# A graph network with a mixture of experts: all rows of the last stage scattered in parts of 40 and 9 tiles, expert weights packed in DRAM, and larger zero fills

## The chip, the cores and the metric

The kernel runs on one core of one Trainium2 chip. The metric is the device time of one execution in microseconds (us), and the figure for a version is the median of its runs. Version before: 4450.49 us, median of three runs between 4450.0 and 4450.73.

## What is computed

The reference takes 6250 nodes with 256 features and a sorted list of 106,250 edges (each node also has an edge to itself). Four blocks follow one another, each of the form x = x + block(layernorm(x)):

```python
x = x + _L0_gnn_ref(_layernorm(x), edge_index, ...)   # two GIN layers, hidden width 512
x = x + _L0_ffn_ref(_layernorm(x)[None], ...)[0]      # slice attention over 64 tokens and 8 heads
x = x + _L1_gnn_ref(_layernorm(x), edge_index, ...)   # one GCN layer with a folded batch norm
x = x + _L1_ffn_ref(_layernorm(x)[None], ...)[0]      # mixture of experts
```

A graph layer sums the rows of the source nodes over the edges of each target node. The mixture of experts is the part that the change is about:

```python
gate_logits = x_flat @ Wg + bg + bias
topk_vals, topk_idx = jax.lax.top_k(gate_logits, TOP_K)          # 2 of 8 experts
topk_w = jax.nn.softmax(topk_vals, axis=-1)
combine = (jax.nn.one_hot(topk_idx, NUM_EXPERTS, dtype=x.dtype) * topk_w[..., None]).sum(axis=1)
h = jax.nn.relu(jnp.einsum('td,edh->teh', x_flat, W1) + b1)      # 256 -> 512
y = jnp.einsum('teh,ehd->ted', h, W2) + b2                       # 512 -> 256
out = jnp.einsum('ted,te->td', y, combine)
```

## The kernel before

The nodes are cut into NT = 49 tiles of 128 rows (the last has 106), the edges into 831 chunks of 128, 17 of them for each tile.

**Sums over edges.** Three times a table in DRAM (T1, T2, T3) holds each node's row as three bf16 pieces. The class `Sums` (L176 to L228) goes over the tiles: for each chunk GpSimd (POOL) issues an indirect DMA that gathers the 128 source rows into a ring of message buffers (L152; 10 buffers in the first and third sum, 32 in the second), with at most `FLIGHT` = 5 on their way, and TensorE (PE) multiplies them with a 0/1 matrix `hot` made by VectorE (DVE, L194), in three matmuls per chunk (L173). Other work is put between these matmuls by hand: `between` gives seven slots per tile.

**Stage 1** (gin1, L635 to L683) is the first sum with the two dense layers of the first GIN layer, for four tiles at a time. Beside it SP, the queue that issues plain DMAs in order, stores the results (S2 at L674, T2 at L680) and fills buffers in DRAM with zeros (L605 to L646): the accumulators S3 and the buffers XD of the experts' rows. Each fill is 512 KB in four slices of one row of zeros per partition, and each waits for a sum that has been added (`added`), so that the fills are spread over the stage.

**Stage 2** (L738 on) is the second GIN layer with the statistics of the attention, then a short dense part. In it `third_needs` (L715) brings the experts' biases b1 into columns and stores them as B1 in DRAM (L728).

**Stage 3** (L965 on) is the GCN sum with the mixture of experts beside it. Its order on SP, PE, ACT and DVE is that of the program text (`manual_schedule`), and `in_order` keeps the order of gathers on POOL. For every two tiles `choice` (L1004) computes the layer's result, normalises it, picks the two experts, and ranks the rows by a matmul with a triangular matrix (pp, L1075), so that each row gets two places in XD, which has a region for each expert. `send` (L1090) scatters the rows there by four indirect DMAs on POOL (L1094). `advance` (L1118) works out on DVE which blocks of 128 rows of one expert are now full, and writes expert and first row of each block into `which`.

A block is fetched by `fetched` (L1170): SP loads two registers from `which`, then issues the loads of xd (128 rows), and by `weights_of` (L1159) those of W1 (512 KB), W2 (512 KB), b1 (2 KB) and b2 (128 KB), up to `AHEAD` = 4 blocks ahead. `block_of` (L1206) transposes xd (L1221), `products` (L1189) does 8 matmuls for the hidden layer (ph, L1195; ReLU with b1 on ACT, L1197) and 4 for the output (py, L1202; b2 added on DVE, L1203), and SP stores the block in its place in XD (L1229). (The profile lists each of these f32 matmuls twice.) A block is done in two slots.

The tiles are divided into parts with XD buffers of their own. When all blocks of a part are done, `combine` (L1253) gathers each row's two results (two indirect DMAs g per tile, L1260, with L152 in the profile) and DVE adds them with their shares (L1265); then the tile goes to `out` (L1002). Parts before: tiles 0 to 35 with 79 blocks and tiles 36 to 47 with 31. How many blocks an expert has is known only when the kernel runs, so the numbers are upper bounds. The last tile is not scattered: it is multiplied with all eight experts ("dense", L1208 to L1217) and each result is added with the row's share, which may be zero.

After the last sum (L1343 on) the remaining blocks follow one another, with one tile combined in each half block.

Of the kernel before, what the change touches and what calls it, by code (L numbers as in the profile page):

```python
# [17 lines left out]
P = 128  # L18
# [3 lines left out]
def gin_transolver_gcn_moe(ctx: ExitStack, tc: tile.TileContext, a: dict, out: bass.AP):  # L22
# [33 lines left out]
    assert C == G == 64 and KD * P == D and KH * P == HID and NT <= P and HID <= 512 and 2 * D <= 512  # L56
# [317 lines left out]
    for upto, size in ((0.75, P), (1.0, P)):  # L374
        ts = [t for t in range(sum(map(len, parts)), NT - 1) if (t + 0.5) / (NT - 1) <= upto]
        if ts:
            parts.append(ts)
            Bs.append(size)
# [4 lines left out]
    zeros = const.tile([P, 1, D], F32, name="zeros")  # L383
# [7 lines left out]
    with tc.tile_pool(name="own", bufs=1) as own:  # L391
# [201 lines left out]
        with tc.tile_pool(name="g1w", bufs=1) as wp, \  # L593
# [12 lines left out]
            for xd in XD:  # L606
                n = xd.shape[0] // P
                for q in range(0, n, 4):
                    m = min(4, n - q)
                    fills.append((xd[q * P:(q + m) * P, :].rearrange("(p j) f -> p j f", p=P), m))  # L610

            for q in range(0, NT, 4):
                m = min(4, NT - q)
                fills.append((S3[q:q + m].rearrange("j p f -> p j f"), m))
# [20 lines left out]
            def gin1(ts):  # L635
                J = len(ts)
                T = J * P
                for t in ts:
                    added = sums1.added
                    for _ in range(-(-len(fills) // (NT - t))):  # L640
                        at, m = fills.pop()
                        ins = nc.sync.dma_start(at, zeros.to_broadcast([P, m, D]))
                        tc.add_manual_dep(ins.ins, added.ins.name,
                                          mybir.DependencyInfo(mybir.DependencyClass.Sync,
                                                               mybir.DependencyReason.DATA),
                                          reason="spread over the stage")  # L646
# [41 lines left out]
    B1 = dram.tile([NE, P, KH], F32, name="B1")  # L688
# [26 lines left out]
    def third_needs(w, ps):  # L715
# [12 lines left out]
        nc.sync.dma_start(B1.rearrange("e p k -> p e k"), b1.rearrange("p (e k) -> p e k", k=KH))  # L728
# [261 lines left out]
    share = keep.tile([P, NE], F32, name="share")  # L990
# [13 lines left out]
    def choice(i, ts, sent_at):  # L1004
# [57 lines left out]
        if i is None:  # L1062
            shares()
            dense.append(xT)
            nc.vector.tensor_scalar(share, pick[0][:, 0, :], sh[:, 0, 0:1], None, op0=OP.mult)
            nc.vector.scalar_tensor_tensor(share, pick[1][:, 0, :], sh[:, 0, 1:2], share, op0=OP.mult, op1=OP.add)
            return


        both = w.tile([P, 4, NE], F32, name="both")  # L1070
        nc.vector.tensor_add(both[:, :J, :], pick[0][:, :J, :], pick[1][:, :J, :])
# [18 lines left out]
    def send(i, ts, xn):  # L1090

        for j, t in enumerate(ts):
            for c in range(2):
                ins = nc.gpsimd.indirect_dma_start(  # L1094
                    out=XD[i], out_offset=bass.IndirectOffsetOnAxis(ap=place[:, t, c:c + 1], axis=0),
                    in_=xn[:, j, :], in_offset=None)
# [62 lines left out]
    def weights_of(e):  # L1159
        W1 = ew.tile([P, KD, HID], F32, name="W1", bufs=AHEAD)  # L1160
        nc.sync.dma_start(W1, a["L1_ffn_W1"][e].rearrange("o (k p) f -> p (o k) f", p=P))
        W2 = ew.tile([P, KH, D], F32, name="W2", bufs=AHEAD)
        nc.sync.dma_start(W2, a["L1_ffn_W2"][e].rearrange("o (k p) f -> p (o k) f", p=P))
        b1 = ew.tile([P, KH], F32, name="b1e", bufs=AHEAD)
        nc.sync.dma_start(b1, B1[e].rearrange("o p k -> p (o k)"))
        b2 = ew.tile([P, 1, D], F32, name="b2e", bufs=AHEAD)
        nc.sync.dma_start(b2[:, 0, :], a["L1_ffn_b2"][e].to_broadcast([P, D]))
        return W1, W2, b1, b2

# [19 lines left out]
    def products(xdT, W1, W2, b1, b2):  # L1189
# [13 lines left out]
        nc.vector.tensor_tensor(yd, p[:, :D], b2[:, 0, :], op=OP.add)  # L1203
        yield yd

    def block_of(i, got):  # L1206

        if i is None:  # L1208
            e, got = got
            it = products(dense[0], *got)  # L1210
            next(it)
            yield
            yd = next(it)
# [170 lines left out]
```

## Time and profile before

The profile comes from one execution with the hardware profiler on, which has a time of its own.

| What | Value |
|---|---|
| Median of the runs without profiler | 4450.49 us |
| Profiled execution: own time | 4515.05 us |
| Profiled execution: span | 4513.4 us |
| Mean granted TensorE clock | 0.817 |
| Stage 1 / stage 2 / attention, about | 100 to 1345 / 1345 to 2700 / 2700 to 2776 us |
| Stage 3: sums / the rest after them | 2776 to 4300 / 4300 to 4513 us |
| Busy: PE, PE loads, DVE, ACT, POOL | 69%, 45%, 34%, 17%, 57% of the span |
| DMA queue q0 (indirect, from POOL) | 182,064 packets, 678.86 MB, 47.8% of 16 engines |
| DMA queue q1 (plain, from SP) | 308,656 packets, 353.08 MB, 24.0% of 16 engines |

A group of instructions is shown as line, engine, operation, what is written and read, shape and count, then busy time in us and the mean of one in ns, then the idle time of the engine before them and what ended it. "PEld" is TensorE loading weights; a name with q (SPq, ACTq) is the engine's own queue of waits and DMA issues, which does not count as busy. "issue" is waiting for nothing that the profile shows. In a timeline each line has start and length in us, and in brackets how long the engine had been idle and for whom. DMA packets are recorded singly in the trace with queue, start, size and duration.

### The profile page before, as it was taken

Reading aid. Unit: us, or ns where it says so; the run is one execution under the profiler, and the core shown is the slowest. Engines: PE = TensorE matmul, PEld = TensorE weight load, DVE = VectorE, ACT = ScalarE, POOL = GpSimd, SP = SyncE. Lnnn points to the kernel's source line nnn. Section 1 sums busy time; section 2 is a strip of 40 time slices with the busy share of each in tenths; the row PEclk is TensorE's granted clock in tenths of the full one; section 3 lists DMA queues with packets and bytes.
Section 4 is the critical chain, followed back from the end, with each engine's and each line's share of the span. In section 5 each row is a group of like instructions: output and inputs, shape, how many; then the busy total and the mean of one; then the engine's idle time right before and its main releaser. Section 6 shows DMA issues by size and latency. Waiting matters only on the chain. (4 is left out here: it accounts for less than half of the span.)

```text
span 4513.4 us, 45778 instructions
## 1 busy us (share of the span) xinstructions
PE 3133.2 (69%) x14516; PEld 2025.4 (45%) x14592; DVE 1532.2 (34%) x3891; ACT 788.2 (17%) x1496; POOL 2578.6 (57%) x2719
## 2 busy tenths in 40 slices
PE   2577777777874777878767876566666666677567
PEld 1233343433442444434434454345555555566456
DVE  6122222222231433433434454333333332333332
ACT  4011111111120111111111123011212221122122
POOL 3666666666646666666666502665665555555642
PEclk6688888888987898988989977677778777788779
DMA  6676666666668888888888755467766676687678
GB/s 210 190 227 215 215 197 206 210 214 208 195 210 289 296 295 301 304 293 289 297 289 292 248 165 178 136 189 220 225 206 207 216 222 215 215 263 219 194 239 257
DMA packets 497447, 1044.56 MB, mean 231 GB/s; under 512 B 79469, under 2 KB 294607, under 8 KB 497200
## 3 DMA queue, kind: packets, MB, share of 16 engines
q0 software_dynamic: 182064, 678.86, 47.8%
q1 hardware_dynamic: 308656, 353.08, 24.0%
q10 hardware_dynamic: 6480, 9.63, 0.6%
q8 instruction: 117, 1.92, 0.2%
q14 instruction: 130, 1.06, 0.1%
HBM read 878.42 MB, written 162.92 MB: 231 GB/s over the span
## 5 line engine op out<-in xcount | busy, mean ns | idle before, releaser
L152 POOL DMA_INDIRECT msg<-T,srcT x2493 | 2359.7, 947 | 1682.4 <-issue 763.0
L173 PE MATMUL pa<-msg,hot 128*128 128x256 bf16 (+2 forms) x7404 | 1492.0, 342 | 540.7 <-DMA msg<-T,srcT 395.1
L173 PEld LDWEIGHTS <-hot 128*128 128x128 bf16 x7479 | 804.8, 108 | 1142.0 <-issue 742.6
L1195 PE MATMUL ph<-xdT,W 128*128 128x128 f32 x1760 | 287.4, 315 | 197.6 <-ACT hT L1197 85.6
L194 DVE SCALAR_TENSOR_TENSOR hot<-dstT,node 128x1152 bf16<-128x1152 f32 (+2 forms) x297 | 373.1, 1258 | 23.8 <-PE pa L173 12.9
L1195 PEld LDWEIGHTS ph<-xdT,W 128*128 128x128 f32 x1760 | 252.8, 219 | 232.5 <-ACT hT L1197 97.5
L1202 PE MATMUL py<-W,hT 128*128 128x256 f32 x944 | 264.9, 425 | 25.4 <-issue 13.8
L622 DVE TENSOR_TENSOR dinv<-dinv,pa 128x1 f32<-128x1 f32 x145 | 22.3, 153 | 714.2 <-PE pa L173 460.8
L1197 ACT ACTIVATE hT<-ph,b1e 128x128 f32<-128x128 f32 x472 | 165.9, 367 | 449.7 <-remote 161.9
L835 PE MATMUL ptok<-xn,sw 128*128 128x257 f32 (+1 forms) x392 | 125.1, 458 | 157.1 <-DVE sw L827 63.7
L670 PE MATMUL p<-W2a,h2T 128*128 128x512 f32 x392 | 199.8, 651 | 33.9 <-issue 18.0
L1202 PEld LDWEIGHTS py<-W,hT 128*128 128x128 f32 x944 | 190.5, 215 | 64.8 <-issue 22.6
L663 PE MATMUL p<-h1T,W1b 128*128 128x512 f32 (+2 forms) x448 | 204.0, 599 | 19.5 <-ACT h1T L657 13.1
L835 PEld LDWEIGHTS ptok<-xn,sw 128*128 128x128 f32 (+1 forms) x392 | 84.8, 227 | 195.7 <-issue 74.7
L152 POOL DMA_INDIRECT g<-XD,place x96 | 93.8, 977 | 125.0 <-DMA XD<-yd 54.8
L1203 DVE TENSOR_TENSOR yd<-py,b2e 128x256 f32<-128x256 f32 x118 | 49.9, 423 | 306.6 <-PE py L1202 177.4
L1015 PE MATMUL pn<-Wg,sT 128*128 128x256 f32 x196 | 82.2, 592 | 83.6 <-issue 44.6
L655 PE MATMUL p<-h0T,W1a 128*128 128x512 f32 (+2 forms) x224 | 129.8, 711 | 7.3 <-issue 4.0
L663 PEld LDWEIGHTS p<-h1T,W1b 128*128 128x128 f32 x448 | 87.5, 212 | 103.8 <-issue 83.2
L670 PEld LDWEIGHTS p<-W2a,h2T 128*128 128x128 f32 x392 | 78.0, 211 | 121.6 <-issue 103.7
L1094 POOL DMA_INDIRECT XD<-xn,place x96 | 94.7, 986 | 62.5 <-issue 46.1
L235 DVE TENSOR_TENSOR s<-s,pa 128x512 f32<-128x512 f32 x49 | 33.6, 685 | 269.0 <-PE pa L173 146.7
(306 smaller groups left out, 3059.6 us busy)
## 6 DMA issues: line engine op xcount, KB each, us to landing
W<-in_L_ffn_W SPq DMA_DIRECT2D x236, 512.0 KB
XD<-zeros SPq DMA_DIRECT2D x100, 512.0 KB
msg<-T,srcT POOLq DMA_INDIRECT x2493
T<-tp SPq DMA_DIRECT2D x49, 384.0 KB
b2e<-in_L_ffn_b SPq DMA_DIRECT2D x118, 128.0 KB
xd<-XD SPq DMA_DIRECT2D x110, 128.0 KB
XD<-yd SPq DMA_DIRECT2D x110, 128.0 KB
S<-s SPq DMA_DIRECT2D x49, 256.0 KB
```

Of the source, the lines that this page charges most:

```text
L152: return nc.gpsimd.indirect_dma_start(out=msg, out_offset=None, in_=table, in_offset=bass.IndirectOffsetOnAxis(ap=ix, axis=0))
L173: nc.tensor.matmul(pa[:, :n], hot, msg[:, s * F:s * F + n], start=(start and s == 2), stop=(stop and s == 1))
L194: nc.vector.scalar_tensor_tensor(hot[:, :n, :], dstT[:, c0:c0 + n, None].to_broadcast([P, n, P]), float(k * HALF), node2[:, k % 2, None, : ...
L655: nc.tensor.matmul(p[:, :T], W1a[:, k, m * P:(m + 1) * P], h0T[:, k, :T], start=(k == 0), stop=(k == KD - 1))
L663: nc.tensor.matmul(p[:, :T], W1b[:, k, m * P:(m + 1) * P], h1T[:, k, :T], start=(k == 0), stop=(k == KH - 1))
L670: nc.tensor.matmul(p, h2T[:, k, j * P:(j + 1) * P], W2a[:, k, :], start=(k == 0), stop=(k == KH - 1))
L835: nc.tensor.matmul(p[:, :D + 1], sws[j][:r, m * P:(m + 1) * P], xn[:r, j, :], start=(j == 0), stop=(j == J - 1))
L1015: nc.tensor.matmul(p[:, :D], sT[:, k, j * P:(j + 1) * P], Wg3[:, k, :], start=(k == 0), stop=(k == KD - 1))
L1094: ins = nc.gpsimd.indirect_dma_start(out=XD[i], out_offset=bass.IndirectOffsetOnAxis(ap=place[:, t, c:c + 1], axis=0), in_=xn[:, j, :], in ...
L1195: nc.tensor.matmul(p[:, :P], W1[:, k, m * P:(m + 1) * P], xdT[:, k, :P], start=(k == 0), stop=(k == KD - 1))
L1197: nc.scalar.activation(hT[:, m, :], p[:, :P], AF.Relu, bias=b1[:, m:m + 1])
L1202: nc.tensor.matmul(p[:, :D], hT[:, m, :], W2[:, m, :], start=(m == 0), stop=(m == KH - 1))
```

## The change

Three things are changed.

First, the parts: all 49 tiles are scattered now, 40 in the first part and 9 in the second, and the dense last tile goes (with it the code for `i is None`). The parts have 87 and 25 blocks. The last tile's 106 rows are ranked, scattered and gathered with slices of 106, and rows past the end are cleared in `both`. What was after the last sum becomes one loop, in which the chains of choices, the last scatters, the blocks and the combining go on side by side.

Second, the weights: in stage 1, for one tile in four, `packed` loads one expert's W1, W2 and b2 (repeated for all partitions) into a buffer and stores it as rows of `EW` = 2308 floats (9,232 bytes) per partition in a DRAM buffer WB. The columns of b1 go to the end of these rows in stage 2, instead of B1. A block's four loads become one load of WB.

Third, the fills: the row of zeros gets four times as long, and each partition fills one contiguous piece of 4 KB instead of four of 1 KB.

```diff
-    for upto, size in ((0.75, P), (1.0, P)):
-        ts = [t for t in range(sum(map(len, parts)), NT - 1) if (t + 0.5) / (NT - 1) <= upto]
+    for upto, size in ((0.81, P), (1.0, P)):
+        ts = [t for t in range(sum(map(len, parts)), NT) if (t + 0.5) / NT <= upto]
...
-    zeros = const.tile([P, 1, D], F32, name="zeros")
+    EW = KD * HID + KH * D + D + KH
+    WB = dram.tile([NE, P, EW], F32, name="WB")
+    zeros = const.tile([P, 4 * D], F32, name="zeros")
...
-                    fills.append((xd[q * P:(q + m) * P, :].rearrange("(p j) f -> p j f", p=P), m))
+                    fills.append((xd[q * P:(q + m) * P, :], m))
...
-                fills.append((S3[q:q + m].rearrange("j p f -> p j f"), m))
+                fills.append((S3[q:q + m].rearrange("j p f -> (j p) f"), m))
+            def packed(e, added):
+                t = w.tile([P, EW - KH], F32, name="wb", bufs=2)
+                for at, ap in (
+                        (t[:, :KD * HID].rearrange("p (k f) -> p k f", f=HID),
+                         a["L1_ffn_W1"][e].rearrange("(k p) f -> p k f", p=P)),
+                        (t[:, KD * HID:EW - KH - D].rearrange("p (k f) -> p k f", f=D),
+                         a["L1_ffn_W2"][e].rearrange("(k p) f -> p k f", p=P)),
+                        (t[:, EW - KH - D:], a["L1_ffn_b2"][e:e + 1].to_broadcast([P, D]))):
+                    spread(nc.sync.dma_start(at, ap), added)
+                nc.sync.dma_start(WB[e][:, :EW - KH], t)
...
-                        ins = nc.sync.dma_start(at, zeros.to_broadcast([P, m, D]))
...
+                        spread(nc.sync.dma_start(at.rearrange("(p j) f -> p (j f)", p=P), zeros[:, :m * D]), added)
+                    if t % 4 == 2 and t // 4 < NE:
+                        packed(t // 4, added)
...
-        nc.sync.dma_start(B1.rearrange("e p k -> p e k"), b1.rearrange("p (e k) -> p e k", k=KH))
+        nc.sync.dma_start(WB.rearrange("e p f -> p e f")[:, :, EW - KH:], b1.rearrange("p (e k) -> p e k", k=KH))
...
-        W1 = ew.tile([P, KD, HID], F32, name="W1", bufs=AHEAD)
-        nc.sync.dma_start(W1, a["L1_ffn_W1"][e].rearrange("o (k p) f -> p (o k) f", p=P))
-        W2 = ew.tile([P, KH, D], F32, name="W2", bufs=AHEAD)
-        nc.sync.dma_start(W2, a["L1_ffn_W2"][e].rearrange("o (k p) f -> p (o k) f", p=P))
-        b1 = ew.tile([P, KH], F32, name="b1e", bufs=AHEAD)
-        nc.sync.dma_start(b1, B1[e].rearrange("o p k -> p (o k)"))
-        b2 = ew.tile([P, 1, D], F32, name="b2e", bufs=AHEAD)
-        nc.sync.dma_start(b2[:, 0, :], a["L1_ffn_b2"][e].to_broadcast([P, D]))
-        return W1, W2, b1, b2
+        wb = ew.tile([P, EW], F32, name="wb", bufs=AHEAD)
+        nc.sync.dma_start(wb, WB[e].rearrange("o p f -> p (o f)"))
...
-    last, = chains
-    for _, *rows in to_send:
-        send(*rows)
-    due.extend(fresh)
-    due.extend((None, e) for e in range(NE))
-    while due or ready or pending[0] is not None:
-        next(last, None)
+    while chains or to_send or due or ready or pending[0] is not None:
+        for it in list(chains):
+            if next(it, chains) is chains:
+                chains.remove(it)
+        if to_send:
+            send(*to_send.pop(0)[1:])
+            new_blocks()
         next(block_pieces)
         if to_combine:
             combine(now[0] + 2)
```

`spread` adds the dependency on `added` that the fills had before. Lines in the profile of the changed kernel are some 3 to 20 higher than before.

## The prediction

> **What bounds the kernel now.** I read the granted clock first (0.817 over the span), then the busy time by stretch, the groups of the last stage, and the timelines of its tail. Columns of the first view: stretch, length, busy us (instructions) of PE, PEld, DVE, ACT, POOL; then clock, DMA share, GB/s.
>
> ```profile
> 400.00:700.00 300.00, 223.26 (x889) 117.96 (x888) 75.05 (x139) 35.48 (x56) 193.68 (x205) 0.85 0.68 210
> 3000.00:3200.00 200.00, 135.83 (x731) 107.80 (x732) 66.81 (x238) 37.78 (x85) 114.47 (x121) 0.75 0.69 213
> 4300.00:4450.00 150.00, 108.47 (x541) 89.40 (x538) 42.75 (x135) 40.35 (x107) 56.46 (x58) 0.81 0.80 247
> ```
>
> No engine is full in stage 1 (100 to 1345 us), the MoE loop (2776 to 4300) or the tail (4300 to 4513). The loop's groups show a coupling instead:
>
> ```profile
> L152 POOL DMA_INDIRECT msg<-T,srcT x829 | 785.1, 947 | 568.4 <-PE pa L173 271.8 <-issue 175.2 <-remote 53.7
> L173 PE MATMUL pa<-msg,hot 128*128 128x256 bf16 x2492 | 433.5, 326 | 224.6 <-DMA msg<-T,srcT 152.0 <-issue 35.6 <-DMA s<-S 21.1
> L1195 PE MATMUL ph<-xdT,W 128*128 128x128 f32 x1424 | 229.2, 312 | 166.3 <-ACT hT L1197 74.7 <-issue 71.7 <-DVE xr L1020 11.4
> ```
>
> POOL waits 272 us for PE to free the ten message buffers, PE 152 us for messages, and 166 us inside expert blocks, mostly behind ACT's ReLU. That ReLU has a wait of its own, for b1's DMA:
>
> ```profile
> L1197 ACTq EVENT_SEMAPHORE x118: 17/1326/10824, 2952.3 to 4495.4; - x118
> ```
>
> Summed over the trace's records it is 208 us for the loop's blocks, 40 us for the tail's. b1 is the fourth of five loads of a block (xd, W1, W2, b1, b2) on SP's queue.
>
> The starts of L1328 give the pace: tile pairs 10 to 39 take 62.3 us on average, with 4 blocks and 38 POOL operations each (34 gathers, 4 scatters; 0.95 us and a 0.30 gap each, 47.5 us). Pairs 40-43 have 7 blocks each and take 61.2 us: three more blocks cost nothing. Pairs 44-47 have 4 blocks, but 14 combining gathers between them, and take 76.3 and 69.1 us. So the loop follows POOL's list, and a block is nearly free in it.
>
> In the tail 29 blocks remain after the last sum at 4300.3: 21 scattered, 8 of the dense last tile. With nothing beside them blocks go at 5.13 us (timeline of PE, then of POOL):
>
> ```profile
> 4442.40 1.99 PE L1202 MATMUL py<-W,hT 128*128 128x256 f32 x8
> 4447.53 1.99 PE L1202 MATMUL py<-W,hT 128*128 128x256 f32 x8
> ...
> 4498.74 1.89 PE L1202 MATMUL py<-W,hT 128*128 128x256 f32 x8
> ```
>
> ```profile
> 4465.18 0.94 POOL L152 DMA_INDIRECT g<-XD,place  x1 [54.76 <-DMA XD<-yd]
> ...
> 4503.66 1.00 POOL L152 DMA_INDIRECT g<-XD,place  x1 [0.30 <-DVE xr L1265]
> ```
>
> The last 24 combining gathers start when the last scattered block's store has landed and run beside the dense blocks; both finish together, near 4500.
>
> **The change, part by part.** Sums are made against the profiled execution (span 4513.4, own time 4515.05). The median without profiler is 4450.49, 1.4% less; I carry the difference in us over unchanged.
>
> *Parts 40 and 9.* Counting the instruction order of both versions: 118 blocks become 112; 88 lie in the loop either way, plus one in the last tile, so the tail falls from 29 to 23. All 98 combining gathers now lie in the tail (before, 18 of 96 lay in tiles 44-48). Pairs 44-47 then have 7 blocks and no combining, as 40-43 had: 145.4 - 2 x 61.2 = **-23 us** (from -10, if the two slow pairs were slow for another reason, to -28 with tile 48's four).
>
> Tail, from the last sum T. The first three blocks end at T+37 before, paced by the last tile's chain; I keep that. The last tile is now scattered. Its ranking matmul follows block 3 (T+36). Placing took 1.5 us on DVE for the previous pair, and from the first scatter to SP's fetch of a final block 14.3 us (4303.5 to 4317.7). So its 16 final blocks can be fetched near T+53 and be there by T+58. Seven blocks, three loaded and four due from pair 46-47, run meanwhile to about T+61: hidden, by 3 us only. Behind the waiting fetch on SP stand the weight loads, output stores and block stores, so a late chain costs its lateness once, 5 to 10 us.
>
> Combining 40 tiles of part one at two per block takes 20 blocks. Such blocks now go at 6.9 us (7 in the 48 us to 4405). SP takes about 7 us for each (eight issues of 0.6, plus 2 of register loads), the DMA engines 6.2 by the packet records. Their undisturbed packets are 46 ns for 1 KB, 84 for 2, 121 for 3, 159 for 4, 178 for 4.6, 234 for 6: a line of 8.5 ns plus 36.7 per KB. Per engine a block's weights are 16 x 84 + 32 x 46 + 8 x 9 + 8 x 46 + 36 = 3.29 us; packed, 8 rows of 9,232 B at an estimated 340 ns, 2.73. With xd and store (0.74) and two tiles' gathers and output (2.18), 5.65 us; at the 92% business of that stretch 6.15. SP falls to five issues, 4.7 us. Then T + 37 + 17 x 6.15 + 3 x 5.13 = T+157. After it nothing hides part two: store 2.5, 18 gathers x 1.25 = 22.5, landing 2.8, add and output 6.5, yd 0.8: 35 us. End T+192 against T+213: **-21 us**. At PE's pace throughout it would be -38, at 6.9 still -8.
>
> *Packed loads in the loop.* Five issues become two; b1 comes with the weights. Its late arrival leaves (up to the 166 us of PE's idle in blocks), but PE's first matmul now waits for the whole 1.18 MB instead of W1's 0.5 MB. Against it speaks the Trainium skill, *DMA: Bandwidth & Descriptors*, section on queues, rings and completion order: a DMA engine takes turns between its queues packet by packet. The trace's gather packets are 4,608 B (178 ns), the loads' 1 and 2 KB (57 ns on average). By the rule gathers get 178/235 = 76% of a contended engine now, and 178/518 = 34% afterwards. A gather is three packets, 0.52 us, per engine: 0.7 us each now, 1.5 us then, above POOL's 1.25. Four block loads in a row (4 x 3.1 = 12.4 us of engine time) would hold gathers for 19 us and put them 2.5 to 3 behind: +3 to +4 us per pair, +75 over 21 pairs. The row says less: in the saturated stretch 3239 to 3266 gathers already took 39.7% of the engines against 51.1% for loads, at about 1.8 us each. They are slow there now, and the stretch gets shorter. Bounds -100 to +75; I take **-12**, near the middle, leaning to the stall that a row shows.
>
> *Zero fills.* 113 fills of 512 KB become 115. Per engine 32 x 46 = 1.47 us becomes 8 x 159 = 1.27: -20 us of DMA time in all. They are 4 KB turns now; one holds a gather for about 1.3 us, and POOL runs up to ten chunks ahead. DVE's longer memset lies in the prologue.
>
> *Packing.* Eight times 3.2 us in and 2.7 out, 47 us of DMA time over tiles 2 to 30 of stage 1, whose DMA share is 0.68. SP's packed store waits for its three loads; behind it stand S2's and T2's stores, which free double buffers that DVE and ACT refill. In the order most of these stores follow an S2 store that waits longer anyway. With the fills, 27 us more DMA work in a stage one third idle: **+4 us** (from -10 to +27). The column of b1 goes to WB with as many rows as before: 0.
>
> Sum: -23 - 21 - 12 + 4 = **-52**: 4398 us.
>
> **Rivals.** *b1 was the brake.* If half of the 166 us vanishes from the pace, POOL's waits for PE shrink as well: 80 rather than 12, giving 4330. For it: 272 us of POOL waiting for PE. Against: pairs 40-43 show that more PE work alone cost nothing. 20%.
>
> *Nothing gained from packing.* Packets may be cut smaller than a row, or SP's long issues are the profiler's; then the tail keeps 6.9 us (-8), the pairs give -10, packing costs 8: 4440. 13%.
>
> *Large packets starve the gathers*, ending slower. By the rule above +75 in the loop, +4 in stage 1, less the 44 of the parts: 4485. It decides once a gather's landing takes longer than five issues, 6.25 us, since five may be on their way; they now land in about 3 us. Twice that in bursts is near, not past it. 12%.
>
> **How the numbers follow.** Likeliest 55%. About 0.2%, 9 us, is what can be told from no change. Faster: nearly all of the likeliest, the first rival, half of the second: 0.80. Same 0.07, slower 0.13. The likeliest case alone spans 4365 to 4430; the range leaves out the slow case and half of the fastest one: 4325 to 4462.
>
> **What would show it.** Queue q1 near 163,000 packets instead of 308,656 and some 1058 MB in all (right packing); ACT's wait at the ReLU short; pairs 44-47 near 61 us; the tail near 192 us, ending in 18 bare gathers, its blocks near 6 us. I am wrong if PE's idle before pa grows past 225 us, if PE waits as long for packed weights as ACT did for b1, if stage 1 is over 15 us longer, or if PE stands still before block 8 of the tail.

## The result, and the profile after

The changed kernel takes **4434.45 us**, median of six runs (4428.25 to 4439.69), against 4450.61 us for the kernel before beside it (4444.54 to 4458.7): ratio 0.9944, 95% interval 0.9923 to 0.9965. By the medians that is 16 us less, by the ratio 25 (16 to 34), where 52 less were forecast. Its profiled execution took 4439.69 us, span 4438.0, mean clock 0.823.

The profile before, on which the sums stand, was an odd base: 4515 us where the other runs took 4450. Five more groups of runs, each on one chip, show that both lengths occur: the kernel before takes 4460 and 4462 us on two chips and 4525 to 4531 us on three others. (Each chip was used once, so the chip and the time of the measurement can't be told apart.) The size of the gain goes with that:

| Chip: median of the kernel before | Changed kernel | Ratio (95%) |
|---|---|---|
| 4450.6 us (the first comparison) | 4434.5 us | 0.9944 (0.9923 to 0.9965) |
| 4462.0 us | 4434.4 us | 0.9925 (0.9904 to 0.9946) |
| 4525.2 us | 4467.4 us | 0.9879 (0.9852 to 0.9906) |
| 4531.4 us | 4469.0 us | 0.9863 (0.9838 to 0.9889) |

So spans are compared below with a second profile of the kernel before, taken on the 4460 chip (span 4458.2):

| Stretch | before (4513 profile) | before (4458 profile) | after (4438) |
|---|---|---|---|
| Stage 1, first to last gather | 1207.5 | 1199.9 | 1200.0 |
| Stage 2, first to last gather | 1232.0 | 1218.2 | 1221.4 |
| MoE loop, first gather to last sum T | 1527.4 | 1482.5 | **1441.3** |
| of it pairs 44-47 | 145.4 | 145.4 | 114.1 |
| Tail, T to the end | 212.9 | 211.1 | **223.7** |

The loop lost 41 us (the prediction had 35), and the tail, which was to lose 21, grew by 13. The other 8 us lie in stage 2 and between the stages, and are no effect that can be told: on the chip of the 4462 the first gather of stage 3 came between 2763.9 and 2778.1 us in four profiles whose code is the same up to there. So differences of some 10 us between single profiles carry little; the loops of these four agree within 3.4 us. The packets came out as worked out: 162,960 on q1 for a forecast of 163,000, and 1058 MB. From the page of after:

```profile
q1 hardware_dynamic: 162960, 366.42, 22.9%
```

The same stretches as before, and the tail (stretch, length, busy us and instructions of PE, PEld, DVE, ACT, POOL; clock, DMA share, GB/s):

```profile
400.00:700.00 300.00, 222.58 (x894) 118.50 (x893) 73.20 (x133) 34.20 (x54) 196.24 (x207) 0.86 0.73 238
3000.00:3200.00 200.00, 137.89 (x816) 111.16 (x815) 70.93 (x250) 44.07 (x99) 121.21 (x128) 0.80 0.69 233
4300.00:4438.00 138.00, 75.70 (x374) 60.19 (x372) 36.19 (x81) 26.28 (x72) 59.53 (x61) 0.79 0.71 232
4260.00:4390.00 130.00, 86.31 (x419) 69.60 (x419) 36.87 (x84) 29.13 (x80) 64.81 (x67) 0.83 0.86 282
```

Stage 1 carries 28 GB/s more, for the packing, with as many matmuls and gathers as before. In the loop's stretch POOL issues 128 operations in 200 us where it issued 121 in the 4513 profile and 126 in the 4458 one. From 4260 to 4390, where blocks and combining lie side by side, PE is busy for 66% of the time, POOL for 50, and the DMA engines for 86: busier than anything else, and still not full.

The loop's groups, first of before (4458 profile), then of after:

```profile
L173 PE MATMUL pa<-msg,hot 128*128 128x256 bf16 x2493 | 430.5, 321 | 246.4 <-DMA msg<-T,srcT 181.5 <-issue 38.6 <-DMA s<-S 22.0
L1195 PE MATMUL ph<-xdT,W 128*128 128x128 f32 x1424 | 227.4, 310 | 156.4 <-issue 72.0 <-ACT hT L1197 43.7 <-DVE xr L1020 32.6
```

```profile
L173 PE MATMUL pa<-msg,hot 128*128 128x256 bf16 x2493 | 439.4, 321 | 306.9 <-DMA msg<-T,srcT 235.9 <-issue 36.7 <-DMA s<-S 21.4
L1208 PE MATMUL ph<-xdT,wb 128*128 128x128 f32 x1424 | 221.6, 307 | 128.5 <-ACT xdT L1226 47.7 <-issue 46.0 <-ACT hT L1210 27.5
```

PE waits 54 us more for messages and 28 us less in blocks; its waits before the combined result (pn) fell by about 60 us. All gaps of PE over 0.15 us went from 525 to 494 us. A wait that grows is no proof of a longer path.

In the tail a stall stands out. PE, then ACT, then POOL, of after:

```profile
4270.76 0.38 PE L1224 MATMUL pt<-ident,xd 128*128 128x128 f32 x2
4283.54 2.07 PE L1208 MATMUL ph<-xdT,wb 128*128 128x128 f32 x8 [12.40 <-issue]
```

```profile
4268.62 0.37 ACT L1210 ACTIVATE hT<-ph,wb 128x128 f32<-128x128 f32 x1 [0.48 <-PE ph L1208]
4283.10 0.38 ACT L1226 ACTIVATE xdT<-pt 128x256 f32<-128x256 f32 x1 [14.11 <-remote]
```

```profile
4268.71 0.94 POOL L152 DMA_INDIRECT g<-XD,place  x1 [0.30 <-issue]
...
4283.11 0.94 POOL L152 DMA_INDIRECT g<-XD,place  x1 [0.30 <-issue]
4292.56 1.07 POOL L152 DMA_INDIRECT g<-XD,place  x1 [8.51 <-DVE xr L1269]
```

PE's transposes for block 7, ACT's input, were done at 4271.1; ACT takes them up 12 us later. The view names no cause ("remote"), but the trace's records hold one: the semaphore by which PE tells the others of its work (a counter that they wait on) is counted up at 4283.02, and ACT starts 0.08 us after that. So ACT was ready, and PE's signal came late. DVE's sum for block 6 starts at 4278.14, again 0.02 us after such a signal, 7.2 us after PE's last matmul of the block. The ends of matmuls are modelled, so the trace does not tell whether PE finished late or its signal was held up. In that time POOL issues gathers with hardly a pause, and SP needs some 0.70 us for about half of its register instructions, which otherwise take 0.02 to 0.3 us and wait for no semaphore. PE stands for 12.4 us, and block 7 follows block 6 after 20.5 us. Later, blocks of 5 to 8 us alternate with some of 9 to 10.

Counted over the last stage of fourteen profiles, from the trace's records, the share of SP's register instructions of 0.55 to 0.9 us depends on how many indirect DMAs POOL has just issued in a row (starts under 1.55 us apart): up to three under 4%, four to six 13%, seven to ten 24%, eleven and more 51%. Message gathers (1.5 KB rows) and combining gathers (1 KB) give the same figures.

The theory from here on: **runs of indirect DMAs on POOL hold up the other engines**, SP in its instructions and ACT and DVE through PE's late signals; two combined tiles a block, four gathers of 1.25 us in a block of 5 us, make the longest runs. Rivals: the last tile's chain is late for block 7; the blocks wait for the DMA engines (bytes, or large packets); DVE, in order, waits for a gather's landing ahead of the block's own sum.

### The profile page after: what moved, and what is told of

It reads as the page before. It is cut to its first block, busy times and chain, and to the rows that moved or that the text cites. A ratio compares the mean times of both kernels' runs of the same rounds, so it can differ in the third digit from the quotient of the medians.

```text
span 4438.0 us, 44258 instructions
## 1 busy us (share of the span) xinstructions
PE 3088.9 (70%) x14455; PEld 1973.5 (44%) x14456; DVE 1532.9 (35%) x3910; ACT 781.9 (18%) x1474; POOL 2593.1 (58%) x2723
## 3 DMA queue, kind: packets, MB, share of 16 engines
q1 hardware_dynamic: 162960, 366.42, 22.9%
## 5 line engine op out<-in xcount | busy, mean ns | idle before, releaser
L173 PE MATMUL pa<-msg,hot 128*128 128x257 bf16 (+2 forms) x7479 | 1507.4, 341 | 637.2 <-DMA msg<-T,srcT 483.3
L1208 PE MATMUL ph<-xdT,wb 128*128 128x128 f32 x1792 | 286.8, 312 | 176.5 <-issue 72.2
L1208 PEld LDWEIGHTS ph<-xdT,wb 128*128 128x128 f32 x1792 | 252.8, 217 | 210.6 <-issue 83.7
L1215 PE MATMUL py<-wb,hT 128*128 128x256 f32 x896 | 245.3, 418 | 30.4 <-ACT hT L1210 21.7
L1210 ACT ACTIVATE hT<-ph,wb 128x128 f32<-128x128 f32 x448 | 160.2, 367 | 396.3 <-PE ph L1208 217.3
L1215 PEld LDWEIGHTS py<-wb,hT 128*128 128x128 f32 x896 | 174.1, 207 | 65.1 <-ACT hT L1210 30.2
L832 PE MATMUL pl<-Weff,xnT 128*128 128x512 f32 x196 | 116.7, 684 | 39.5 <-issue 33.1
L1111 POOL DMA_INDIRECT XD<-xn,place x98 | 98.6, 1006 | 75.9 <-issue 23.7
L811 PE MATMUL p<-W2b,h4T 128*128 128x256 f32 x392 | 119.7, 402 | 24.5 <-issue 21.9
L1216 DVE TENSOR_TENSOR yd<-py,wb 128x256 f32<-128x256 f32 x112 | 47.5, 424 | 256.0 <-PE py L1215 129.8
```

The source lines that it names most:

```text
L173: nc.tensor.matmul(pa[:, :n], hot, msg[:, s * F:s * F + n], start=(start and s == 2), stop=(stop and s == 1))
L811: nc.tensor.matmul(p[:, j, :], h4T[:, k, j * P:(j + 1) * P], W2b[:, k, :], start=(k == 0), stop=(k == KH - 1))
L832: nc.tensor.matmul(p, xnT[:, k, j * P:(j + 1) * P], Weff[:, k, :], start=(k == 0), stop=(k == KD - 1))
L1208: nc.tensor.matmul(p[:, :P], W1[:, k, m * P:(m + 1) * P], xdT[:, k, :P], start=(k == 0), stop=(k == KD - 1))
L1210: nc.scalar.activation(hT[:, m, :], p[:, :P], AF.Relu, bias=b1[:, m:m + 1])
L1215: nc.tensor.matmul(p[:, :D], hT[:, m, :], W2[:, m, :], start=(m == 0), stop=(m == KH - 1))
```

## The experiments

Times in the tail are from T, the end of the last sum. "Last py" is the end of the last block's matmuls; pace is from block 4's py to block 23's, divided by 19.

### The parts of the change alone (chip with before at 4460)

`a1_before`: no edit.

> The kernel before, unchanged, profiled a second time. The profile on which the prediction was built took 4515 us, the kernel's other runs 4444 to 4459. If that execution was an odd one, this profile's own time is near 4450, and the lines on which the sums stood shrink: the pairs 44-47 then cost less than 145 us together, and the loop (2773 to the last sum) less than 1527 us. If a profile always costs such 65 us, it is near 4515 again and the sums stand.

4458.85 us, profile 4459.88. So a profile does not cost 65 us, and the first one was most likely taken on a slower chip: its stage 2 (1232.0 us) lies among the 1223 to 1236 of the profiles on those chips, not among the 1216 to 1225 of the others. Pairs 44-47 took 145.4 us here too, so that term stood.

`a2_parts`: the changed kernel with the old loads and fills.

```diff
-        wb = ew.tile([P, EW], F32, name="wb", bufs=AHEAD)
-        nc.sync.dma_start(wb, WB[e].rearrange("o p f -> p (o f)"))
+        W1 = ew.tile([P, KD, HID], F32, name="W1", bufs=AHEAD)
+        nc.sync.dma_start(W1, a["L1_ffn_W1"][e].rearrange("o (k p) f -> p (o k) f", p=P))
...
-                    if t % 4 == 2 and t // 4 < NE:
-                        packed(t // 4, added)
```

> Only the parts of 40 and 9 with all rows scattered; five loads a block and fills in 1 KB pieces as before. By the prediction's own sum it gives the -23 of pairs 44-47 and of the tail's -21 what doesn't hang on the lighter loads (-8): about 4420. Rival A (the pairs 44-47 were slow in one odd execution only, and the tail's combining is no cheaper): 4440 to 4450. Rival B (packing costs time and hides a gain of the parts): below 4420.

4438.74, ratio 0.9941 (0.9923 to 0.9959): -26 us by the ratio, -22 by the medians. Loop 1458.2 (-24), pairs 44-47 113.2 (-32), but tail 220.5 (+9). The loop's term came and the tail's did not, without any packing.

`a3_packing`: the kernel before with `packed`, WB and one load a block.

> Only the packing: weights and biases packed in stage 1, one load per block; parts and fills as before. The prediction: -12 in the loop, up to -13 in the tail by lighter blocks, +8 in stage 1, about 4433. Rival B (packets of 9 KB put the gathers behind): 4460 or more, with PE's idle before pa grown in the loop. Rival C (b1's late landing was hidden anyway): 4450, ACT's wait gone and turned into a wait of PE for wb.

4440.84, ratio 0.9956 (0.9940 to 0.9973), -20 us: loop -9.5, tail 198.5 (-12.6), stage 1 +3.9. The forecast's terms were -12, -13 and +8. But the two parts alone add up to 46 us by the ratios (42 by the medians), and together they give 25 to 33 (16 to 28).

`a4_fills`: the kernel before with 4 KB fills.

> Only the zero fills in 4 KB pieces; everything else as before. The prediction puts it between -4 and 0 (20 us of DMA work less in a stage that is one third idle): 4447 to 4450. If 4 KB turns hold the gathers in stage 1: stage 1 grows by 5 us or more. If stage 1 follows its DMA work after all: -10 or more.

4457.42, ratio 0.9995 (0.9973 to 1.0016); stage 1 1200.1 against 1199.9 us. No effect that can be told, though 20 us of DMA time is gone.

### The combining in the tail (chip with before at 4462)

`b0_after`: no edit.

> The changed kernel once more, beside the same runs of the kernel before as its variants. Alone, the parts gave 0.9941 and the packing 0.9956. If the two gains add, 0.990 here (4416 against 4460). If the first result holds (0.9944), the second gain is lost where the two meet: loop near -41 us against the kernel before, tail +9 to +13.

0.9925: the gains don't add. Loop 1439.1, tail 219.5; so it is the tail in which the packing's gain is lost.

`b1_late_combine`: all 98 gathers after the last block.

```diff
         next(block_pieces)
-        if to_combine:
-            combine(now[0] + 2)
         run_ends()
```

> The changed kernel with all 98 combining gathers after the last block, none beside blocks. Theory M (runs of POOL's gathers hold up the other engines' instructions): blocks go at 5.1 to 5.3 us, the stall before block 7 shrinks below 5 us, SP's control instructions of 0.7 us vanish from the blocks; last py at T+141 to T+148, then 98 gathers x 1.25 + 12 us: end T+275 to T+285, 55 us slower than the changed kernel (4490). Rival C (block 7 waits for the last tile's chain, as the prediction had it): the stall of 10 us or more stays, last py at T+155 or later, end near T+292. Rival D (the blocks wait for 9 KB packets whatever POOL does): blocks stay above 6 us, last py at T+160 or later.

4465.23, ratio 1.0005 (0.9985 to 1.0025). Last py at T+124.8 against T+182.8, pace 5.2 us with 4.9 for most blocks, and block 4 at T+24 instead of T+38. Before the last py the changed kernel has 80 gathers (12 of them ahead of the last scatters), this one 8. So 72 gathers cost 58 us beside the blocks, where they cost 90 bare (1.25 us each): the overlap hides a third of them, not nearly all. Without them nothing holds PE, at full clock:

```profile
4260.00:4330.00 70.00, 61.62 (x378) 51.96 (x378) 5.94 (x14) 27.09 (x74) 0.00 (x0) 1.00 0.77 271
```

A gap of 10 us before block 7 remained here, not long after eight gathers in a row; `c3_pool_busy` below has none, so it isn't the chain. The third block ends at T+21 in both, at T+34 to T+37 in the changed kernel: what paced its first blocks were the twelve gathers in front, and not the last tile's chain.

`b2_half_combine`: one combined tile a block.

```diff
-        if to_combine:
+        if to_combine and now[0] % 2 == 0:
             combine(now[0] + 2)
```

> The changed kernel with one combined tile a block instead of two. Theory M: POOL issues two gathers and pauses, runs longer than six vanish, blocks at 5.2 to 5.5 us, last py near T+145; the 52 gathers left then take 65 + 12 us: end near T+222, 4434 as before. Rival D (bytes and packets): the slowing is proportional, 6.3 us a block, last py near T+163, end T+240, 4450. Rival L (DVE's queue in order, waiting for landings): as D, since each combine still stands in DVE's queue.

4424.17, ratio 0.9912 (0.9878 to 0.9946). Last py at T+143.3 (the theory said T+145, the rival by bytes T+163), tail 213.5. Block 7 still comes 11.4 us after block 6, then the blocks go at 4.9, and at the end at 5 to 7: pace 5.9, between the theory's 5.5 and the rival's 6.3. With 52 gathers before the last py it costs 18 us against b1, and the 28 more of the changed kernel cost 40: not proportional.

`b3_deep_g`: 14 buffers for g, sums four pieces later.

```diff
-            g = w.tile([P, D], F32, name="g", bufs=8)
+            g = w.tile([P, D], F32, name="g", bufs=14)
...
-            combine(now[0] + 2)
+            combine(now[0] + 4)
```

> The changed kernel with 14 buffers for the combining gathers in place of 8, and their sums on DVE four pieces later in place of two. Rival L (DVE waits for a gather's landing ahead of the block's own sum, and POOL for DVE: 38.5 us of POOL's idle): POOL's wait for DVE falls below 10 us, blocks at 6 us or less, last py at T+160, 4408. Theory M: POOL runs on in longer runs, the other engines' instructions slow as much or more; blocks no faster than 7 us, last py T+175 to T+190, 4425 to 4440.

4444.00, ratio 0.9953 (0.9935 to 0.9971): not faster. Last py at T+192, 25.9 us from block 6 to block 7. More buffers let POOL run on (22 DMAs in a row at most, 20 in b0), and the stall grew. But POOL's wait for DVE stayed at 42 us (39 in b0), where the rival wanted less than 10, so this run does not rule out DVE's order. `c4_tiny_gathers` below does: nothing on DVE waits for its tiny gathers, and the stall is larger.

### What it is about the gathers (chip with before at 4530)

`c2_three_gathers`: three gathers a block, none before the last scatters.

```diff
-        if to_combine:
+        if to_combine and not to_send and not chains and now[0] % 4:
             combine(now[0] + 2)
```

> The changed kernel with three combining gathers a block on the mean (three tiles in two blocks) and none before the last tile's scatters are issued. If only long runs hurt (six in a row, then a pause): blocks at 5.3 to 5.8 us, last py near T+135, the 40 gathers left cost 50 + 12 us: end near T+197, 4410. If every gather above two a block costs as much as a bare one (1.25 us): end near T+213 as with two a block, 4424.

4449.73, ratio 0.9812 (0.9781 to 0.9842), on a chip where the changed kernel itself was not run. Last py at T+156, not T+135; pace 6.8; tail 209.1. My price for runs of six was too low; 66 gathers before the last py cost 31 us, the last 14 of them, against b2, some 0.9 each. Still this is the shortest tail of all versions with the new parts.

The next three keep all combining for after the last block, as `b1_late_combine` does, and put work that nothing uses beside the blocks, in the places of the changed kernel's gathers. Each of them has one execution alone, the profiled one, so their times carry no interval.

```diff
+            busy = w.tile([P, 1216], F32, name="busy", bufs=1)                  # c3_pool_busy, two a piece
+            in_order(nc.gpsimd.iota(busy, pattern=[[1, 1216]], base=0, channel_multiplier=0, ...))
...
+            gt = w.tile([P, 16], F32, name="gt", bufs=8)                        # c4_tiny_gathers, two a piece
+            in_order(gather(gt, tiny, slot_i[:, 0:1]))
...
+        gt = w.tile([P, 2, D], F32, name="gt", bufs=4)                          # c5_bytes_from_sp, one a piece
+        nc.sync.dma_start(gt, a["x"][now[0] % 24 * 2 * P:(now[0] % 24 + 1) * 2 * P, :].rearrange("(j p) f -> p j f", p=P))
```

> The kernel with all combining after the last block, and 92 iotas of some 1.2 us on POOL where the changed kernel has gathers (12 ahead of the last scatters, the rest beside blocks): POOL is as busy, but issues no DMA. They are additional work and compute nothing that is used. Theory M1 (it takes indirect DMAs): blocks stay at 4.9 us, no SP instruction of 0.7 us in the blocks; last py near T+125 (later by what the last scatters wait for the twelve). Theory M2 (a busy POOL is enough): blocks at 6 us or more, SP's control instructions of 0.7 us.

Last py at T+122.0, blocks at 4.9, block 7 5.0 us after block 6, none of SP's 205 register instructions at 0.7 us. The stretch has POOL at 94% and PE untouched:

```profile
4300.00:4370.00 70.00, 59.91 (x365) 50.12 (x364) 5.95 (x14) 26.09 (x71) 66.04 (x59) 1.00 0.86 297
```

It also shows that the last tile's chain is hidden, as the prediction said with "3 us only".

> As the one before, with 92 indirect gathers of 64-byte rows in place of the iotas: as many descriptors as the combining gathers have, a sixteenth of their bytes; additional work that is not used. Theory M1 (the issue of indirect DMAs in runs): the blocks slow to 6.5 us or more while POOL runs, SP's control instructions take 0.7 us, block 7 waits 10 us or more. Theory M3 (the gathers' bytes in the DMA engines): blocks stay near 4.9 us.

The blocks all but stop: 56 us from block 6 to block 7 and 60 us from 7 to 8, then 4.9 us a block as soon as the tiny gathers are through, last py at T+243.7. The windows, while POOL issues 80 gathers in a row, 72 of them tiny:

```profile
4300.00:4350.00 50.00, 5.93 (x22) 4.31 (x21) 0.42 (x1) 1.49 (x4) 37.74 (x40) 0.53 0.25 72
4350.00:4412.00 62.00, 7.98 (x23) 5.63 (x23) 0.42 (x1) 1.85 (x5) 37.75 (x40) 0.50 0.16 45
```

The DMA engines are at 0.16 to 0.25, so it is neither bytes nor bandwidth. ACT's timeline shows one instruction in 11 us, in a group of four that otherwise follow one another in 0.4 to 0.9:

```profile
4331.73 0.37 ACT L1214 ACTIVATE hT<-ph,wb 128x128 f32<-128x128 f32 x1 [10.80 <-remote]
4342.88 0.37 ACT L1214 ACTIVATE hT<-ph,wb 128x128 f32<-128x128 f32 x1 [10.78 <-remote]
4353.38 0.37 ACT L1214 ACTIVATE hT<-ph,wb 128x128 f32<-128x128 f32 x1 [10.13 <-issue]
```

Here too ACT's instruction was there: before 4331.73 its wait instruction stands for 11.12 us, and in the first two lines the semaphore is counted up less than 0.08 us before ACT starts, 8.7 and 9.5 us after the end of PE's matmuls. Over all 22 blocks, ACT takes up a block's transposes 0.10 us after their end in b1 and c3; the longest such delay is 10 to 12 us in the four profiles of the changed kernel and 26.7 us here. Fetching of instructions does not show as the cause, with one refill in these 112 us:

```profile
q14 instruction: 1, 0.01, 0.0%
```

> As the one before, with the same bytes as the combining gathers (256 KB per piece, two pieces a block, rows of 1 KB) loaded by SyncE's queue in place of POOL; additional work that is not used. Theory M3 (bytes): blocks at 6 to 7.5 us as in the changed kernel. Theory M1: blocks at 4.9 to 5.6 us (a DMA share near 0.8), no stall of 10 us before block 7 beyond the 5 of the kernel with late combining.

Last py at T+140.9, block 4 at T+23.7, from there 6.1 us a block, and no stall (7.7 us between blocks 6 and 7). SP has as many issues a block as in the changed kernel. The DMA engines are nearly full, and the blocks go on:

```profile
4280.00:4368.00 88.00, 69.49 (x384) 57.31 (x382) 6.37 (x15) 27.33 (x74) 0.00 (x0) 0.94 0.96 334
```

My limit of 5.6 us for the theory was too low: bytes do cost something. Last py is 16 us later than with no gathers at all. The changed kernel also stores the combined rows, 128 KB a tile, some 5 MB beside its blocks: at 334 GB/s 15 us more, as an estimate. That leaves 27 to 31 of the 58 to 62 us for the runs, about 14 of them ahead of block 4. So a busy POOL is harmless, bytes cost about half by this estimate, and the rest is put down to the issue of indirect DMAs in runs, which with hardly any bytes can all but stop the other engines. That both causes exist is shown; how the loss divides between them is worked out by difference, and no run isolates it.

### Packing with short runs (chip with before at 4525)

> The changed kernel a third time, as the measure for the three below in the same session. If the gain does not depend on the chip: 0.992 to 0.995 of the kernel before. If the slow first profile of the kernel before (4515) was of such a session as the last one (before 4530), the gain in such a session may be larger, up to 0.985.

`d0_after` (no edit): 0.9879, -58 us by the medians, the changed kernel's largest gain so far, with the tail as long as ever (223.5; 229.2 in `e0_after` below).

> One combined tile a block again, now beside the changed kernel. Theory M1: tail of 210 to 215 us against 220 to 224; 8 to 12 us (0.2%) faster than the changed kernel. If its first result was chance: the same as the changed kernel.

`d1_half_combine` (the edit of b2): 4458.40, ratio 0.9855 (0.9825 to 0.9884); tail 213.5 to the tenth as in b2. It is 9 us below the changed kernel, and the intervals overlap.

`d2_half_unpacked`: the edit of b2 on `a2_parts`.

> The parts alone (five loads a block, fills in 1 KB pieces) with one combined tile a block. It tells where the packing's gain lies once POOL's runs are short. If five loads hold the blocks (SyncE's issues and b1's landing, as the prediction had it): blocks at 5.8 to 6.5 us against 4.9 to 5.2, tail 15 to 25 us longer than with packed loads. If loads never were the limit of the tail: the same tail within 5 us.

4506.98, ratio 0.9950 (0.9930 to 0.9970), runs from 4466 to 4545. Against d1 the tail is 11 us longer (last py T+154.3 against T+143.2), less than the 15 to 25 expected of loads that hold the blocks, and the **loop 60 us** (1514.8 against 1455.0). The profile of d2 (4530) lies near the slow end of its runs; by the medians the two differ by 49 us in all. On this kind of chip the packed loads are most of the gain. From 3200 to 4000 us, d2 and then d1:

```profile
3200.00:4000.00 800.00, 533.68 (x3055) 433.46 (x3053) 275.87 (x994) 158.92 (x361) 465.10 (x488) 0.77 0.69 215
```

```profile
3200.00:4000.00 800.00, 552.34 (x3213) 443.90 (x3211) 285.96 (x1031) 169.15 (x381) 486.71 (x511) 0.80 0.67 225
```

Unpacked, every engine does 2 to 6% less in the 800 us, at a lower clock and with a slightly higher DMA share.

`d3_half_seven_msgs`: d1 with seven message buffers.

```diff
-    sums = Sums(T3, msgs, 10, hots, ps, add3)
+    sums = Sums(T3, msgs, 7, hots, ps, add3)
```

> One combined tile a block, and seven message buffers in the last stage instead of ten, so that POOL cannot run ten gathers in a row there. If the runs of gathers also hold the MoE loop up: SP's control instructions of 0.7 us fall below 4% in the loop and the loop is 10 to 30 us shorter. If the loop needs the lookahead: PE waits longer for messages, the loop 15 us or more longer.

4460.28, ratio 0.9862 (0.9829 to 0.9895), the same as d1; loop 1458.4. SP's slow instructions in the stage fell from 86 to 62, PE's wait before pa rose, and neither moved the time. A miss for both expectations.

### The twelve gathers ahead of the last scatters (chip with before at 4531)

> The changed kernel beside the last variant, in one session. Where the kernel before takes 4450 to 4465, a ratio of 0.992 to 0.9945; where it takes 4525 to 4530, 0.986 to 0.990. Anything between would say that the size does not go with the session.

`e0_after` (no edit): 0.9863, so the gain is again the larger where the kernel before is slow.

`e1_half_after_sends`:

```diff
-        if to_combine:
+        if to_combine and not to_send and not chains and now[0] % 2 == 0:
             combine(now[0] + 2)
```

> One combined tile a block, and none before the last tile's six scatters are issued (the changed kernel issues 12 gathers there). Theory M1: the last tile's own chain is not held up either, so block 4 comes at T+24 as with late combining (T+40 in the changed kernel), last py near T+133, the 52 gathers left take 70 us: end near T+203, 10 us less than with one tile a block from the start and 20 less than the changed kernel. If gathers beside that chain cost nothing: T+213, as without this edit.

4460.11, ratio 0.9846 (0.9819 to 0.9874). Block 4 comes at T+24.4 as expected (T+37 in e0), last py at T+139.3, but more gathers are left for the end: tail 216.8, not 203. The six gathers moved from ahead of that chain bring the last py 4 us forward and cost 7 us at the end, so moving them gains nothing. Of the versions that ran beside the changed kernel, b2, d1 and e1 are the best; each is 9 or 10 us below it, with overlapping intervals.

## Where the prediction was right, and where it failed

**Pairs 44-47: -23.** Right, and more: -31 (145.4 to 114.1), and -32 with the parts alone. Pairs 40-43 took 8 us more than in the 4458 profile (127.3 against 119.2), so the eight tiles together gained 23.

**Packed loads in the loop: -12.** About right on the faster chips: -9.5 alone, and -10 to -18 as what is left of the 41 after the pairs. On the slower chips it is several times that (60 us between the profiles of d2 and d1). The bounds of -100 to +75 held both. The rule that speaks against it (the Trainium skill, *DMA: Bandwidth & Descriptors*, queues, rings and completion order) showed in its direction at most: PE's wait for messages grew by 54 us, and it did so with the packing (211 us in a3) and not with the parts (180 in a2). But the price of +75 did not come, since waits elsewhere on PE fell by more. Gather packets kept their mean duration in the loop (257 ns in both), so the stall that the rule priced did not show in them (a gather's three packets are 2 x 178 + 121 = 477 ns undisturbed, not the 0.52 us of the sum, which changes little). A block's loads took about 0.6 us less of a DMA engine (forecast 0.56).

**b1's landing.** I read ACT's wait of 208 us as b1's landing. Its line in after, for 112 blocks:

```profile
L1210 ACTq EVENT_SEMAPHORE  x112: 17/1348/10596, 2954.1 to 4396.5; - x112
```

The wait is still 185 us for the loop's 89 blocks, against 208 and 226 in the two profiles before. An undisturbed block of the tail shows 1.16 us of it, the time from xdT's end to PE's first result; 89 of these are 103 us that were never b1's. The first rival (b1 the brake, 4330) stood on that misreading and fell.

**Stage 1: +4.** Within a few microseconds: 0 in the profile of after, +3.5 and +3.9 in b0 and a3; the fills by themselves did nothing.

**The tail: -21, measured +13.** This is the step that failed: "With xd and store (0.74) and two tiles' gathers and output (2.18), 5.65 us; at the 92% business of that stretch 6.15", and from it "T + 37 + 17 x 6.15 + 3 x 5.13 = T+157". T+37 was right in its number (37.3) by luck: it was not the last tile's chain that paced these blocks, for without gathers beside them (b1, c3) the third block ends at T+21. The last three blocks were right (5.1 each), the 35 us at the end were 36.7. The step that failed is the 6.15 us: the seventeen blocks beside combining took 134 us instead of 105, 7.9 us each. The prediction priced them by the DMA engines' work and put what POOL's gathers do to the other engines at nothing. Two things make up the 29, in sizes that are estimates:

- *The DMA term was too small.* In the records of after, a DMA engine works some 6.6 us per block there (about 113 us over 17 blocks), not 5.65. I had taken the undisturbed durations; beside each other packets take longer on the mean: 430 ns for 9,232 B (estimate 340, median 348), 218 for the 4,096 B of the combining gathers (159). At 0.96 of the engines, which c5 reached, a block takes 6.9 us: 17 x 0.75 = 13 us, as an estimate.
- *POOL's runs*, the remaining 16, by difference: four gathers take all of an undisturbed block's 5.1 us, so that POOL has no pause left, and its runs (up to 16 in a row) hold up SP, and ACT and DVE through PE's late signals. The 20.5 us before block 7 alone are 15 more than a block.

The gaps also cost clock. From block 4 to block 20 PE itself is busy for 5.36 us a block in after and for 4.46 in b1, at a mean clock of 0.83 and 0.96; that is 14 of the 45 us between the two. The clock stands at half in seven stretches between T+20 and the last py, and each begins where PE was busy for at most 0.44 of the 4 us before, as in the stall before block 7:

```profile
4276.50:4290.20 13.70, 5.22 (x20) 4.67 (x21) 2.18 (x5) 1.74 (x5) 5.65 (x6) 0.50 0.62 188
4290.20:4314.10 23.90, 16.91 (x98) 13.48 (x96) 8.74 (x20) 6.55 (x18) 14.60 (x16) 1.00 0.97 318
```

So the lower clock follows the gaps here and is part of their price; no run separates it.

I had seen 6.9 us a block in the tail before, with the same runs in it, and put all of it down to SP and DMA. Packing relieves both, so it shortens the tail where combining is lighter (a3: -12.6; d1 against d2: -11) and hardly where two tiles go beside each block (after 223.7, b0 219.5, a2 220.5). That this is the reason is argued, not shown.

The last tile's chain, "hidden, by 3 us only", was hidden (c3). The sign I gave for its failure, PE standing before block 8, appeared in the stall before block 7, for another reason. PE's idle before pa also grew past the 225 us that I had named as a sign of being wrong, and the loop was shorter nonetheless.

**The base.** The sums were made on an execution that fits a slower chip, and carried over to a median of a faster one. On chips like the profile's, the change gives -58 and -62, near the forecast of -52, but that is luck: a loop gain of 82 us where 35 were forecast (1527.4 to 1445.2 in the profiles) covers the tail's loss there too. Why five loads a block are so much dearer on those chips stays open: the profiles show only a lower clock and fewer operations in the same time, and not which of the two leads.

The second rival's time (4440) was nearest, by luck and not for its reason: the packets were not cut, and the loads did get shorter.

## What to carry to other kernels

Price work that is laid "beside" other work by what its issue does to the other engines too, and look for instructions and signals that come late without a cause that the view names. Keep runs of indirect DMAs on POOL short where other engines have much to do: here the first two a block cost some 0.4 us each, and the next two 1.4 each, more than the 1.25 of one alone (b1, b2 and b0). Size a DMA term with the mean duration of packets under load, not with the undisturbed one, and take a second profile of the kernel before, on another chip, before a sum of a few tens of microseconds is built on one.

## What was not expected of the hardware

- A run of indirect DMAs on POOL holds the other engines up: 51% of SP's register instructions take some 0.7 us from the eleventh DMA on, against under 4% without a run, and PE's signals come up to 12 us after its matmuls in the changed kernel; with 80 gathers in a row, 72 of them of 64-byte rows, ACT did one instruction in 11 us. It looks as if instructions arrived late, but the Trainium skill (*Runtime: NRT & Kernel Launch*, instruction fetch mechanics) has fetching mostly hidden, and the trace agrees in so far as it has one refill in the 112 us of these stalls and shows ACT's instruction waiting for PE's signal. What holds the signal up stays open.
- POOL's price of a gather doesn't depend on its bytes: 0.94 us and 0.30 of gap for rows of 64 bytes, 0.95 and 0.30 for rows of 1 KB.
- Rows of 9,232 bytes go as single packets, 350 ns at the median (8.5 + 9.0 x 36.7 = 339 by the line through the smaller ones).
- The medians on five chips and in the first comparison differ by up to 1.8% for the kernel before, and by up to 0.8% for the changed one, which ran on three of the chips.
